# A hand-ordered prologue becomes one ordered by readiness, with its loads and eleven filler pieces regrouped

## The chip, the cores and the metric

The kernel runs on one core of one Trainium2 chip. The metric is the device time of one execution in microseconds (us); less is better. The core has a matrix engine (PE, whose weight loads are listed apart as PEld), a vector engine (DVE), an activation engine (ACT), a general engine (POOL) and a queue that issues most transfers (SP). Each engine works through its own instructions in the order fixed when the program is built, and waits where an operand is not there yet.

## The reference

x holds 32 sequences of 64 rows of 256; ctx_1024 holds 32 contexts of 1601 rows of 256. Six layers are added to x one after the other. Cut to what matters here:

```
x = x + L0_xattn(layernorm(x), ctx)   # x1 @ W1.T + (mean of ctx over its 1601 rows) @ W2.T + b
x = x + L0_attn(layernorm(x))         # attention of 64 by 64, 16 heads of 16, slopes * (j - i) added to the scores
x = x + L0_ffn(layernorm(x))          # shared gated network, and routed experts
x = x + L1_xattn(layernorm(x), ctx)   # 16 heads: softmax(q k^T / 4) v with k, v = Wk ctx + bk, Wv ctx + bv
x = x + L1_attn(layernorm(x))         # convolution, gated recurrence, gated network
x = x + L1_ffn(layernorm(x))          # ternary weights, 8-bit activations
```

Most of the work is in L1_xattn: each context row becomes a key and a value and is scored against 64 queries in 16 heads.

## The kernel before

**Tiles and pieces.** Two sequences make a tile of 128 rows, so there are 16 tiles (NT), taken in the order 1 to 15 and then 0. For L1_xattn each tile is split into 13 pieces (NU): per sequence (b) and per half of the channels (oc) three pieces of 512 context rows, and one piece with the 65 rows that are left of all four ("rest"). The main loop (L1463) runs over all 208 pieces g. One pass of it does, among others: `column_scores(g)` (L894, scores with context rows on partitions, exponential on ACT), `values(g + 3)` (L844), `row_scores(g + 5)` (L855, scores with queries on partitions, only to find the maxima, which DVE reduces, L871 and L874), `weighted(g)` (L924, the sum over values) and `keys(g + 6)` (L768, evicted by ACT with the bias added, L779 and L789). In the row-score order of a tile the rest piece comes first (number 0). `maxima` (L876) and `maxima_rows` (L887) turn the maxima of a half into a row of negative shifts that the column scores need. Between these, the layers of other tiles are run in small steps (generators that yield) from a plan with due times.

**Prologue.** Before the loop the first pieces must be there: keys 0 to 5, values 0 to 2, row scores 0 to 4, and for the row scores the query of the first tile, which needs the tile's whole first layer. `first()` (L1369) gives this chain in 27 steps: normalisation, the sums of two contexts (on ACT and DVE; L1377 to L1388), L0_xattn (xat, L359 to L365), L0_attn (transposed input tp_b, keys, queries and values, L375 to L403; scores, softmax, L408 to L433; weighted sum and wo, L446 to L479), L0_ffn (su, sv, lg, so, L486 to L505) and the query (tp_d, q, qbd, L746 to L764). Beside it stand the context sums of tiles 1 to 3 (`early_sums`, L1400: loads of 800 KB into two buffers "part", each summed by ACT), the second tile's first layer (`besides`, four effective steps), and the loads of the later weights (`late_weights`, L1247).

**What sets the order.** The prologue and the loop are inside `tc.manual_schedule` (L1430) for PE, DVE, ACT and POOL: there each engine's instructions stand in the order in which the program writes them. The prologue's order is a string of letters: a is one step of the chain, s of the sums, b of the second tile, k, v and r are keys, values and row scores of a piece, m and t the first maxima, w the late weights.

```
for what in """a a a a k1 a a k2 a a s s k3 k0 a a a a s s s s a k4 a v0 v1 a a a s s s s s s b a b a b a b a s w
               a s s a a a b a a s s s r b r b s s s r k5 b r m s s s r v2 t""".split():
    do[what]()
```

What is written outside that block (constants, masks, memsets, the first loads) and everything on SP is ordered on each engine by the compiler: among the instructions that its model takes to be ready, the one written first goes first.

**Buffers and queues.** PSUM has three single buffers for general results (mm_tile), two double ones for scores (sc_tile) and one for the weighted sums (o_tile). Key tiles have 7 buffers, contexts 2. The loads stand on SP's queue, in the text's order keys' weights, x, context 0, L0_xattn's weights, context 1 (two transfers), rest, eight weights; ACT's queue has the vectors chv, the rows (six bias rows and slopes, spread over 128 partitions) and the values' weights.

Of the kernel before, what the change touches and what calls it, by code (L numbers as in the profile page):

```python
# [15 lines left out]
P = 128  # L16
NB = 32
S = 64
# [26 lines left out]
def perceiver_kernel(ctx: ExitStack, tc: tile.TileContext, a: dict, out: bass.AP):  # L45
# [38 lines left out]
    def mm_tile(shape, name, dtype=F32):  # L84
        return home[0].mm.tile(shape, dtype, tag="mm", name=name)
# [38 lines left out]
    def load_rest(ti):  # L124

        t = big.tile([P, 2, 2, TAIL], F32, tag="rest", name=f"rest_{ti}", bufs=2)
        for b in range(2):
            nc.sync.dma_start(t[:, :, b, :], a["ctxT"][2 * ti + b].rearrange("(c p) l -> p c l", p=P)[:, :, NP * PIECE:])
        return t
# [2 lines left out]
    chv = const.tile([P, 2, len(CH)], F32, name="chv")  # L132
    nc.scalar.dma_start(chv, a["chv"])
    rows = const.tile([P, R_END], F32, name="rows")
    nc.scalar.dma_start(rows, a["rows"].partition_broadcast(P))

    ident = const.tile([P, P], F32, name="ident")
    make_identity(nc, ident)
# [26 lines left out]
    for hb in range(2):  # L165
        nc.gpsimd.iota(dist[hb * S:(hb + 1) * S, :], pattern=[[1, S]], base=0, channel_multiplier=-1,
                       allow_small_or_imprecise_dtypes=True)
    albi = const.tile([P, H, S], F32, name="albi")
    nc.vector.tensor_tensor(albi, rows[:, R_SL:R_SL + H].unsqueeze(2).to_broadcast([P, H, S]),
                            dist.unsqueeze(1).to_broadcast([P, H, S]), ALU.mult)  # L170


    gains = const.tile([P, 2, 3], F32, name="gains")
# [2 lines left out]
    def load_w(name, cols, chunks=2, eng=None):  # L176
        t = const.tile([P, chunks, cols], F32, name=f"w_{name}")
        (eng or nc.sync).dma_start(t, a[name].rearrange("(c p) o -> p c o", p=P))
        return t
# [588 lines left out]
    def keys(g):  # L768

        pos, h, k = scanned(g)  # L770
        if h is None:
            w = wholes[pos]
            w.kt = big.tile([P, 4, TAIL], F32, tag="ktr", name=f"ktr_{w.ti}", bufs=2)
            o = mm_tile([P, 2, 2 * TAIL], f"kps_{w.ti}")
            for oc in range(2):
                mmq2(o[:, oc, :], lambda c: w_k2[:, c, oc * P:(oc + 1) * P],
                     lambda c: w.rest[:, c].rearrange("p b l -> p (b l)"))
            for oc in range(2):
                nc.scalar.activation(w.kt.rearrange("p (b o) l -> p o b l", o=2)[:, oc],  # L779
                                     o[:, oc, :].rearrange("p (b l) -> p b l", b=2), AF.Identity,  # L780
                                     bias=chv[:, oc, BK2:BK2 + 1])
            return
        hf = halves[h]
        kt = big.tile([P, PIECE], F32, tag="kt", name=f"kt_{hf.name}_{k}", bufs=7)
        hf.kt.append(kt)
        o = mm_tile([P, PIECE], f"kps_{hf.name}_{k}")
        cT = ctxs[hf.batch]
        mmq2(o, lambda c: w_k2[:, c, hf.oc * P:(hf.oc + 1) * P], lambda c: cT[:, c, k * PIECE:(k + 1) * PIECE])
        nc.scalar.activation(kt, o, AF.Identity, bias=chv[:, hf.oc, BK2:BK2 + 1])  # L789
# [35 lines left out]

    def half_values(pos, h, k):
        v = value_tile([((pos, h, k), range(4))])
        o = mm_tile([P, 4, P], f"vps_{h}_{k}")
        cT = ctxs[h // 2]
        for j in range(4):  # L830
            k0 = k * PIECE + j * P
            mm2(o[:, j, :], lambda c: cT[:, c, k0:k0 + P], lambda c: w_v2[:, c, h % 2 * P:(h % 2 + 1) * P])
        values_out(v, o, P)
# [42 lines left out]
    def maxima(h):  # L876

        hf = halves[h]
        ng = small.tile([P, 4], F32, tag="ng", name=f"ng_{hf.name}")
        nc.vector.tensor_reduce(ng, wholes[hf.pos].mx[:, :, h % 4, :], AX.X, ALU.max, negate=True)  # L880
        m = mxp[h % 2]
        nc.vector.tensor_copy(m[:, :, 0], ng)
        nc.vector.tensor_tensor(ng, ng, m[:, :, 0], ALU.subtract)
        nc.vector.tensor_copy(m[:, :, 1], ng)
        nc.vector.tensor_tensor(m[:, :, 2], ng, m[:, :, 1], ALU.subtract)
# [327 lines left out]
    def load_batch(n):  # L1213
        hf = halves[2 * n]
        ctxs[n] = load_ctx(2 * hf.ti + hf.b, n == 1)


    w_k2 = load_w("L1_xattn_WkT", D)
    early_x[order[0]] = load_x(order[0])
    load_batch(0)  # L1220
    w_v2 = load_w("L1_xattn_WvT", D, eng=nc.scalar)
    w_xat = load_w("L0_xattn_WT", D, 4)
    load_batch(1)
    wholes[0].rest = load_rest(order[0])
    w_k = load_w("L0_attn_WkT", D)
    w_q = load_w("L0_attn_WqT", D)
    w_v = load_w("L0_attn_WvT", D)
# [129 lines left out]
    def first_layer(pos, k=0):  # L1357
        x3[pos] = yield from layer0(order[pos], csums.get(pos), k)
# [41 lines left out]
    def early_sums():  # L1400
        for pos in range(1, 4):
            yield from sums(pos, 2)
# [3 lines left out]
    def planned(gen, t0, t1, n, place):  # L1406
        plan.append(Steps(gen, t0 * NU / 16, t1 * NU / 16, n, place))
# [19 lines left out]
    planned(queried(NT - 1), 226, 231, 6, 2)  # L1427

    ET = mybir.EngineType
    with tc.manual_schedule(engines={ET.PE, ET.DVE, ET.Activation, ET.Pool}):  # L1430
        ahead, beside, summing = Steps(first()), Steps(first_layer(1, 1)), Steps(early_sums())

        def besides():
            if 1 in csums:
                beside.step()

        def scored():
            row_scores(scores.pop(0))

        scores = list(range(5))  # L1440
        do = {"a": ahead.step, "b": besides, "s": summing.step, "r": scored, "w": late_weights, "m": lambda: maxima(0),
              "t": lambda: maxima_rows(0)}
        do |= {f"k{g}": lambda g=g: keys(g) for g in range(6)} | {f"v{g}": lambda g=g: values(g) for g in range(3)}

        for what in """a a a a k1 a a k2 a a s s k3 k0 a a a a s s s s a k4 a v0 v1 a a a s s s s s s b a b a b a b a s w
                    a s s a a a b a a s s s r b r b s s s r k5 b r m s s s r v2 t""".split():
            do[what]()
        if beside.gen is not None:
            plan.insert(0, Steps(beside.gen, 0, 4, 28 - beside.done, 2))
        planned(biased(), 3, 5, 2, 1)  # L1450
        if summing.gen is not None:
            plan.insert(0, Steps(summing.gen, 0, 4.5, 37 - summing.done, 0))
        planned(all_ternary(), 5, 23, 24, 2)

        def run(t, place):
            for s in [s for s in plan if s.t0 <= t]:
                s.run(t, place)
                if t >= s.t1 and t < NU * NT - 1 and s.stop is None:
                    s.all()
                if s.gen is None:  # L1460
                    plan.remove(s)

        for g in range(NU * NT):  # L1463
            pos, p = divmod(g, NU)
            if pos + 1 < NT:
                if p == 0:
                    wholes[pos + 1].rest = load_rest(order[pos + 1])
                if p in (2, 9):
                    load_batch(2 * pos + 2 + p // 8)
            column_scores(g)  # L1470
            if g + 4 < NU * NT and scanned(g + 4)[2] == NP - 1:
                maxima_rows(scanned(g + 4)[1])
            if g == NU:
                more_values()
            if g + 3 < NU * NT:
                values(g + 3)
            if p == 1 and pos:
                normalise(pos - 1)
            if g == NU * NT - 2:
                normalise(pos, 3)  # L1480
            run(g, 0)
            if g + 5 < NU * NT:
                row_scores(g + 5)
                if scanned(g + 5)[2] == NP - 1:
                    maxima(scanned(g + 5)[1])
            run(g, 0.5)
            weighted(g)
            if p == NU - 1 and pos < NT - 1:
                gathered(pos)
            if p == 3 * NP and pos == NT - 1:  # L1490
                gathered(pos, 3)
            if g == NU * NT - 5:
                picked()
            in_columns[0] = True
            if g + 6 < NU * NT:
                keys(g + 6)
            if p == 1 and pos:
                x4[pos - 1] = projected(pos - 1)
            run(g, 1)
            in_columns[0] = False  # L1500
        normalise_last(NT - 1)
        x4[NT - 1] = projected(NT - 1)
        loop.close()
        late = []
        for k in range(2):
            late.append(Home(ctx.enter_context(tc.tile_pool(name=f"late{k}", bufs=2)),
                             ctx.enter_context(tc.tile_pool(name=f"late{k}s", bufs=3)),
                             ctx.enter_context(tc.tile_pool(name=f"late{k}m", bufs=3 - k, space=PSUM))))
        main = home[0]
        home[0] = late[0]  # L1510
        home[0].padded()
# [52 lines left out]
```

## Time and profile before

| | us |
|---|---|
| median of 3 runs | 2029.11 (2028.45 to 2029.33) |
| the profiled execution | 2027.19 |
| its span (first to last instruction) | 2025.5 |
| PE busy in the span | 1942.1 (96%) |
| DVE, ACT, POOL busy | 1295.2, 900.4, 326.4 |
| first column scores start | 77.4 |
| PE busy before that | 51.94 |

Times in the profile count from the span's start. The span is 1.7 us shorter than the execution's own time. A row of the timeline gives start, duration, engine, line, operation, what is written and from what, its shape and how many instructions were merged; in brackets stands how long the engine was idle before it and what ended the wait. PE's granted clock is given per stretch of time, 1.00 being full speed.

### The profile page before, as it was taken

How to read it: one execution, taken by the hardware profiler on the slowest of the kernel's cores; microseconds unless marked ns; L12 is line 12 of the kernel's file. 1: busy time of each engine (PE TensorE's matmuls, PEld its weight loads, DVE VectorE, ACT ScalarE, POOL GpSimd, SP SyncE). 2: the span in 40 equal slices, each digit the busy share in tenths (PEclk: the TensorE clock that was granted, in tenths of full speed). 3: DMA queues.
4: the chain of work that ended last, by engine and by line, in shares of the span. 5: the costliest groups of instructions: out<-in, count | busy, mean ns of one | idle time of the engine just before them, and what ended most of it. 6: DMA issues, size and time to landing. Idle time of an engine off the chain costs nothing. (4 is left out here: it accounts for less than half of the span.)

```text
span 2025.5 us, 76418 instructions
## 1 busy us (share of the span) xinstructions
PE 1942.1 (96%) x35143; PEld 1290.7 (64%) x35143; DVE 1295.2 (64%) x2618; ACT 900.4 (44%) x1400; POOL 326.4 (16%) x548
## 2 busy tenths in 40 slices
PE   6889999999999999999999999999999999999986
PEld 4556566667666666666666666666766666666664
DVE  4556766666656766666666766666666776656555
ACT  4345445454645444354544434444343433434342
POOL 2112111121111112111111111112111011100011
PEclk9899999999999999999999999999999999999998
DMA  9235323122232112121211111100111210111000
GB/s 310 78 117 168 122 86 112 48 79 84 89 99 87 56 48 73 66 78 64 72 48 54 43 50 40 50 28 25 35 51 45 81 45 2 48 47 38 13 10 8
DMA packets 54793, 136.68 MB, mean 67 GB/s; under 512 B 13318, under 2 KB 35016, under 8 KB 54472
## 3 DMA queue, kind: packets, MB, share of 16 engines
q1 hardware_dynamic: 53912, 130.99, 19.1%
q8 instruction: 275, 4.51, 0.9%
q10 hardware_dynamic: 560, 0.81, 0.2%
q14 instruction: 46, 0.38, 0.1%
HBM read 125.53 MB, written 6.25 MB: 65 GB/s over the span
## 5 line engine op out<-in xcount | busy, mean ns | idle before, releaser
L921 ACT ACTIVATE pt<-s 128x1024 f32<-128x1024 f32 (+1 forms) x416 | 403.1, 1020 | 266.6 <-PE s L915 266.4
L874 DVE TENSOR_REDUCE mx<-r 128x2 f32<-128x1024 f32 x384 | 451.8, 1219 | 97.1 <-PE r L867 96.8
L789 ACT ACTIVATE kt<-kps,chv 128x512 f32<-128x512 f32 x192 | 132.0, 687 | 581.9 <-PE kps L265 564.2
L253 PE MATMUL vps<-w_L_xattn_WvT,ctxT 128*128 128x256 f32 (+1 forms) x1632 | 380.4, 377 | 2.1 <-DVE y L1046 1.8
L265 PE MATMUL kps<-ctxT,w_L_xattn_WkT 128*32 128x512 f32 x2992 | 355.3, 592 | 0.0
L253 PEld LDWEIGHTS vps<-w_L_xattn_WvT,ctxT 128*128 128x128 f32 x1632 | 281.9, 190 | 48.3 <-issue 2.2
L867 PE MATMUL r<-kt,qbd 32*128 32x512 f32 x1536 | 231.5, 647 | 2.8 <-DVE mx L874 2.0
L814 DVE COPY vau<-vps 128x512 f32<-128x512 f32 x142 | 97.9, 690 | 203.5 <-PE vps L253 202.9
L940 PEld LDWEIGHTS o<-pt,vau 128*32 128x32 f32 (+1 forms) x9792 | 147.4, 110 | 97.4 <-issue 86.0
L915 PE MATMUL s<-qbd,kt 32*128 32x128 f32 x6144 | 208.1, 270 | 0.0
L915 PEld LDWEIGHTS s<-qbd,kt 32*128 32x128 f32 x6144 | 205.4, 186 | 3.0
L940 PE MATMUL o<-pt,vau 128*32 128x64 f32 (+1 forms) x9792 | 173.9, 221 | 3.8 <-ACT pt L921 3.5
L265 PEld LDWEIGHTS kps<-ctxT,w_L_xattn_WkT 128*32 128x32 f32 x2992 | 83.3, 110 | 112.0 <-issue 112.0
L867 PEld LDWEIGHTS r<-kt,qbd 32*128 32x128 f32 x1536 | 68.7, 184 | 46.4 <-issue 29.0
L909 PE MATMUL s<-neg,onesb 3*128 3x512 bf16 x768 | 82.4, 384 | 5.8 <-DVE mx L874 4.9
L909 PEld LDWEIGHTS <-onesb 3*128 3x128 bf16 x768 | 21.3, 91 | 104.0 <-issue 101.9
L814 DVE COPY part<-vps 128x512 f32<-128x512 f32 x50 | 34.5, 691 | 70.5 <-PE vps L253 70.3
L940 PEld LDWEIGHTS o<-pt,part 128*32 128x32 f32 (+1 forms) x3520 | 54.0, 110 | 34.9 <-issue 30.3
L311 ACT ACTIVATE part<-part 128x1601 f32<-128x1601 f32 x48 | 74.1, 1544 | 1.7 <-DMA part<-ctxT 1.7
L940 PE MATMUL o<-pt,part 128*32 128x64 f32 (+1 forms) x3520 | 65.4, 220 | 1.4 <-ACT nT L1054 0.7
L389 POOL TENSOR_TENSOR kbd<-kT,mask 128x512 f32<-128x512 f32 x32 | 32.6, 1040 | 114.0 <-ACT kT L382 114.0
L253 PE MATMUL ff<-nT,w_fg 128*128 128x128 f32 x384 | 48.7, 276 | 2.3 <-DVE fm L274 1.6
(391 smaller groups left out, 2517.5 us busy)
## 6 DMA issues: line engine op xcount, KB each, us to landing
ctxT<-ctxT SPq DMA_DIRECT2D x31, 1601.0 KB
part<-ctxT SPq DMA_DIRECT2D x60, 800.5 KB
od<-osb SPq DMA_DIRECT2D x15, 256.0 KB
rest<-ctxT SPq DMA_DIRECT2D x32, 65.0 KB
x<-x SPq DMA_DIRECT2D x16, 128.0 KB
out<-x SPq DMA_DIRECT2D x16, 128.0 KB
w<-w SPq DMA_DIRECT2D x16, 128.0 KB
rs<-od SPq DMA_DIRECT2D x30, 64.0 KB
```

Of the source, the lines that this page charges most:

```text
L253: nc.tensor.matmul(o, lhsT=lhsT(c), rhs=rhs(c), start=(c == 0), stop=(c == 1))
L265: nc.tensor.matmul(o[r], lhsT=lhsT[:, r], rhs=rhs, start=start, stop=stop)
L311: nc.scalar.activation(parts[j], parts[j], AF.Copy, accum_out=csum[:, c, 2 * i + b:2 * i + b + 1])
L389: nc.gpsimd.tensor_tensor(kbd[oc], kT[:, oc, :].rearrange("p (b k) -> p b k", b=2).unsqueeze(2).to_broadcast([P, 2, 4, S]), mask4.unsqueez ...
L789: nc.scalar.activation(kt, o, AF.Identity, bias=chv[:, hf.oc, BK2:BK2 + 1])
L814: nc.vector.tensor_copy(v[:kr, :, 0:VW - 16].rearrange("p k (h d) -> p k h d", d=17)[:, :, :, 0:16], o[:kr].rearrange("p k (h d) -> p k h ...
L867: nc.tensor.matmul(o, lhsT=qbd[r, q % 2, q // 2].rearrange("p h q -> p (h q)"), rhs=w.kt[r, q, :] if h is None else halves[h].kt[k][r, :], ...
L874: nc.vector.tensor_reduce(w.mx[:, 2 * m:2 * m + 2, h % 4, k], ps[m], AX.X, ALU.max)
L909: nc.tensor.matmul(o, lhsT=onesb[r, :], rhs=halves[h].neg[r, :].unsqueeze(1).to_broadcast([3, 4, P]), start=True, stop=False)
L915: nc.tensor.matmul(ps[i // 2][:kr, i % 2, j * P:(j + 1) * P], lhsT=w.kt[r, j, :] if h is None else halves[h].kt[k][r, j * P:(j + 1) * P], ...
L921: nc.scalar.activation(pt[:kr].rearrange("p i k c -> p i (k c)"), ps[m][:kr], AF.Exp)
L940: nc.tensor.matmul(w.o[32 * c:32 * c + 32, q, m, :], lhsT=v[:kr, i, 17 * hd:17 * hd + 32], rhs=pts[m][:kr, c // 2, j, c % 2 * S:c % 2 * S ...
```

## The change

The prologue's steps are written ahead of `tc.manual_schedule`, so that they are ordered by readiness, and the loop alone stays in the hand-ordered block. In the text the whole chain (27 steps) stands first, then keys 1, 2, 3, 0, 4, 5, values 0 to 2, row scores 0 and 1, keys 6, row scores 2, keys 7, row scores 3, the first maxima; then 13 steps of the sums, 4 of the second tile, the late weights and 9 more steps of the sums. Keys 6 and 7 are new in the prologue and left out of the first two passes of the loop. Row scores 4 move into the first pass, ahead of `weighted(0)`, which now stands ahead of row scores 5. Keys before piece 6 use the score buffers instead of the general ones, and values 0 to 2 the buffer of the weighted sums. The first loads are x, context 0, L0_xattn's weights, context 1, then the keys' weights, the rows but for their first 256 columns (which stay on ACT's queue), the values' weights (moved from ACT's queue to SP's) and the rest; albi, the table of slopes times distances, is computed after these in the text.

```
-    nc.scalar.dma_start(rows, a["rows"].partition_broadcast(P))
+    nc.scalar.dma_start(rows[:, 0:R_BO], a["rows"][0:R_BO].partition_broadcast(P))
...
-            o = mm_tile([P, 2, 2 * TAIL], f"kps_{w.ti}")
+            o = sc_tile(f"kps_{w.ti}")[:, :, :2 * TAIL] if g < 6 else mm_tile([P, 2, 2 * TAIL], f"kps_{w.ti}")
...
-        o = mm_tile([P, PIECE], f"kps_{hf.name}_{k}")
+        o = sc_tile(f"kps_{hf.name}_{k}")[:, 0] if g < 6 else mm_tile([P, PIECE], f"kps_{hf.name}_{k}")
...
-        o = mm_tile([P, 4, P], f"vps_{h}_{k}")
+        o = o_tile([P, 4, P], f"vps_{h}_{k}") if 3 * h + k < 3 else mm_tile([P, 4, P], f"vps_{h}_{k}")
...
-    w_k2 = load_w("L1_xattn_WkT", D)
     early_x[order[0]] = load_x(order[0])
     load_batch(0)
-    w_v2 = load_w("L1_xattn_WvT", D, eng=nc.scalar)
     w_xat = load_w("L0_xattn_WT", D, 4)
     load_batch(1)
+    w_k2 = load_w("L1_xattn_WkT", D)
+    nc.sync.dma_start(rows[:, R_BO:], a["rows"][R_BO:].partition_broadcast(P))
+    w_v2 = load_w("L1_xattn_WvT", D)
     wholes[0].rest = load_rest(order[0])
+    albi = const.tile([P, H, S], F32, name="albi")
...
+    for what in """a a a a a a a a a a a a a a a a a a a a a a a a a a a k1 k2 k3 k0 k4 k5 v0 v1 v2 r r k6 r k7 r m t
+                s s s s s s s s s s s s s b b b b w s s s s s s s s s""".split():
+        do[what]()
...
     with tc.manual_schedule(engines={ET.PE, ET.DVE, ET.Activation, ET.Pool}):
...
             run(g, 0)
+            if g == 0:
+                scored()
+                weighted(g)
             if g + 5 < NU * NT:
                 row_scores(g + 5)
...
-            weighted(g)
+            if g:
+                weighted(g)
...
-            if g + 6 < NU * NT:
+            if 7 < g + 6 < NU * NT:
                 keys(g + 6)
```

More of the change, by code (lines that the diff above doesn't have):

```diff
@@ L167, in perceiver_kernel @@
                        allow_small_or_imprecise_dtypes=True)
-    albi = const.tile([P, H, S], F32, name="albi")
-    nc.vector.tensor_tensor(albi, rows[:, R_SL:R_SL + H].unsqueeze(2).to_broadcast([P, H, S]),
-                            dist.unsqueeze(1).to_broadcast([P, H, S]), ALU.mult)
     gains = const.tile([P, 2, 3], F32, name="gains")
@@ L1215, in load_batch @@
         ctxs[n] = load_ctx(2 * hf.ti + hf.b, n == 1)
-    w_k2 = load_w("L1_xattn_WkT", D)
     early_x[order[0]] = load_x(order[0])
     load_batch(0)
-    w_v2 = load_w("L1_xattn_WvT", D, eng=nc.scalar)
     w_xat = load_w("L0_xattn_WT", D, 4)
     load_batch(1)
+    w_k2 = load_w("L1_xattn_WkT", D)
+    nc.sync.dma_start(rows[:, R_BO:], a["rows"][R_BO:].partition_broadcast(P))
+    w_v2 = load_w("L1_xattn_WvT", D)
     wholes[0].rest = load_rest(order[0])
+    albi = const.tile([P, H, S], F32, name="albi")
+    nc.vector.tensor_tensor(albi, rows[:, R_SL:R_SL + H].unsqueeze(2).to_broadcast([P, H, S]),
+                            dist.unsqueeze(1).to_broadcast([P, H, S]), ALU.mult)
     w_k = load_w("L0_attn_WkT", D)
@@ L1429, in perceiver_kernel, with besides, scored @@
     ET = mybir.EngineType
-    with tc.manual_schedule(engines={ET.PE, ET.DVE, ET.Activation, ET.Pool}):
[L1431 to L1453, printed above, removed]
+    ahead, beside, summing = Steps(first()), Steps(first_layer(1, 1)), Steps(early_sums())
+    def besides():
+        if 1 in csums:
+            beside.step()
+    def scored():
+        row_scores(scores.pop(0))
+    scores = list(range(5))
+    do = {"a": ahead.step, "b": besides, "s": summing.step, "r": scored, "w": late_weights, "m": lambda: maxima(0),
+          "t": lambda: maxima_rows(0)}
+    do |= {f"k{g}": lambda g=g: keys(g) for g in range(8)} | {f"v{g}": lambda g=g: values(g) for g in range(3)}
+    for what in """a a a a a a a a a a a a a a a a a a a a a a a a a a a k1 k2 k3 k0 k4 k5 v0 v1 v2 r r k6 r k7 r m t
+                s s s s s s s s s s s s s b b b b w s s s s s s s s s""".split():
+        do[what]()
+    if beside.gen is not None:
+        plan.insert(0, Steps(beside.gen, 0, 4, 28 - beside.done, 2))
+    planned(biased(), 3, 5, 2, 1)
+    if summing.gen is not None:
+        plan.insert(0, Steps(summing.gen, 0, 4.5, 37 - summing.done, 0))
+    planned(all_ternary(), 5, 23, 24, 2)
+    with tc.manual_schedule(engines={ET.PE, ET.DVE, ET.Activation, ET.Pool}):
         def run(t, place):
```

## The prediction

> **What bounds the kernel now.** I read the page first (engine shares, then the 40 slices), then a table of busy time by stage, then the first 130 us in order of time, then the waits. The slices (about 50.6 us each) show PE at 6 and 8 tenths in the first two and 9 until the last two: the kernel is bound by PE except in a prologue and a tail. The diff touches only the prologue and the first two pieces of the loop. The table by stage (PE, PEld, DVE, ACT, POOL busy, then the granted clock, DMA share and GB/s) is cut at the loop's first column scores (77.4) and the next three:
>
> ```profile
> 0.00:77.40 77.40, 51.94 (x299) 31.95 (x300) 39.30 (x76) 28.05 (x46) 15.03 (x42) 0.82 0.72 243
> 77.40:89.30 11.90, 11.22 (x169) 8.02 (x169) 4.30 (x7) 3.51 (x6) 1.84 (x4) 1.00 0.01 3
> 89.30:98.40 9.10, 9.10 (x191) 5.94 (x191) 5.04 (x8) 4.07 (x6) 2.83 (x3) 1.00 0.28 92
> 111.00:1950.00 1839.00, 1808.55 (x33736) 1199.06 (x33736) 1195.06 (x2393) 834.30 (x1282) 287.65 (x468) 1.00 0.19 62
> ```
>
> The loop is 98% PE (1808.55 of 1839) and stays as it is. So the change is worth (1) how much earlier the first column scores start and (2) what the first two pieces gain or lose. What ends last before 77.4 is one chain: contexts loaded and summed, tile 0's first layer, its query, row scores, maxima, first column scores. Its PE steps (start, duration), with idle time ahead in brackets:
>
> ```profile
> 11.91 3.75 PE L261 MATMUL kps<-ctxT,w_L_xattn_WkT 128*128 128x512 f32 x4 [11.91 <-DMA ctxT<-ctxT]
> 19.74 1.13 PE L261 MATMUL xat<-w_L_xattn_WT,mT 128*128 128x256 f32 x4
> 43.52 2.08 PE L253 MATMUL su<-xT_c,w_L_ffn_sw1T 128*128 128x128 f32 x8 [0.46 <-ACT xT_c L243]
> 48.32 2.05 PE L261 MATMUL so<-w_L_ffn_sw2T,m 128*128 128x256 f32 x4 [0.37 <-PE lg L261]
> 56.71 2.08 PE L867 MATMUL r<-ktr,qbd 32*128 32x65 f32 x32 [0.45 <-DVE qbd L761]
> 59.58 2.68 PE L867 MATMUL r<-kt,qbd 32*128 32x512 f32 x8 [0.79 <-DVE mx L871]
> 62.98 3.20 PE L867 MATMUL r<-kt,qbd 32*128 32x512 f32 x8 [0.72 <-DVE mx L874]
> 66.11 3.55 PE L261 MATMUL kps<-ctxT,w_L_xattn_WkT 128*128 128x512 f32 x4
> 72.27 2.26 PE L867 MATMUL r<-kt,qbd 32*128 32x512 f32 x8 [1.32 <-DVE mx L874]
> 74.45 2.05 PE L253 MATMUL vps<-w_L_xattn_WvT,ctxT 128*128 128x128 f32 x16
> ```
>
> Two things are to be seen. Durations double where PE was idle before: a key piece is 3.75 at 11.9 and 3.55 at 66, but 1.88 at 20.7; the granted clock reads 0.50 from 42 to 69. And behind the query (56.7) the hand order still puts a key piece (66.11) and a value piece (74.45) into the chain.
>
> **A. Start of the chain.** It is gated by the second context's sums:
>
> ```profile
> 17.30 0.99 DVE L1387 TENSOR_REDUCE csum<-ctxT 128x1 f32<-128x801 f32 x1 [3.69 <-DMA ctxT<-ctxT]
> ```
>
> Ahead of and with that load the kernel requests 4892 KB (14 + 524 rows + 256 keys' + 256 values' weights + 128 x + 1601 + 512 + 1601). After the change 3984 KB: 908 KB fewer (396 of the rows, 256, 256). At the 374 GB/s of 10 to 20 us that is 2.5 us. ACT's last part sum began 0.91 us after the landing, because an eviction and a copy stood before it; with the keys gone from there, that goes too. So xat could start at 19.74 - 3.4 = 16.3. But no keys have warmed PE: four matmuls of that shape take 2.05 cold (so) against 1.13, +0.9. **A = -2.5.** Ends: -3.4, if PE is warm; +0.4, if the first key piece (its weights land 0.7 us later, at 15.5) is queued whole ahead of xat (15.5 + 3.75 = 19.25, plus 0.9). I lean to the early end: xat needs 1.5 us after the landing. The rows' remainder, the values' weights and albi (1.22 us of DVE, at 7.9 now) move to a time when DVE waits for loads; both DMAs stand ahead of the layer weights on SP's queue, 652 KB or 1.8 us, and those are first read 5 us after xat: nothing.
>
> **B. xat to query (20.98 to 56.71).** *Gain:* all keys and three values are now fillers behind the chain, ordered by readiness: 7 x 1.88 + 1.06 + 3 x 2.05 = 20.4 us of PE work. Chain work on PE from xat to tp_c is 9.2 us, cold start 3: together 16.3 + 32.6 = 49, so PE can stay busy and warm until so. Warm prices are the second tile's: su to lg takes 1.89 there (116.12 to 118.01) against 3.57, so 1.03 (xat's row) against 2.05, transpose and query 1.6 against 2.74. Gain 1.7 + 1.0 + half of 1.15 = 3.3. *Loss:* the hand order let the chain wait for almost no filler; an order by readiness starts a filler just before the chain's next step is ready. PE: 12 entries, half meet a 0.47 us matmul, half of it left: 1.4. ACT: 8 evictions of 0.69 and about 3 sums of 1.73 are 10.7 us in 36, 30%; 8 entries x 0.3 x 0.45 = 1.1. **B = -3.3 + 2.5 = -0.8**; ends -3.8 (all warm, no delay) and +5.5 (each of the eight evictions ahead of a step). Key pieces now evict from the score buffers and values from the output buffer, idle until the loop: nothing, and if one is late it is a filler that is late.
>
> **C. Query to first column scores (56.71 to 77.42, 20.7 us).** Gone from here: the key piece, the fifth row scores, the value piece. I replay the rest with the cold rows: row scores start 56.71, 59.58, 62.98; the next needs the first maximum of the third (ends 66.3) instead of following the key piece at 69.8. Their second maxima end 4.5 us after the start, as in the 62.98 row (67.46): 70.8. Five small maxima 1.0, transpose 0.2 plus copy and gaps 0.5: column scores at 72.5. **C = -4.9.** If PE were warm, four row scores at the 2.46 spacing of 69.81 to 72.27 would give -9.4; if both key pieces stay between row scores, as the text has them, 0.
>
> **D. First pieces.** Two key pieces leave (1.90 each) and one row scores comes in (1.14). That looks like -2.7, but the rows of the first piece say otherwise:
>
> ```profile
> 83.55 2.34 DVE L874 TENSOR_REDUCE mx<-r 128x2 f32<-128x1024 f32 x2
> 84.34 1.90 PE L265 MATMUL kps<-ctxT,w_L_xattn_WkT 128*32 128x512 f32 x16
> 85.80 0.41 DVE L219 TENSOR_SCALAR xn_b<-x,mv_b,rstd_b 128x256 f32<-128x256 f32 x1
> 86.35 0.41 PE L237 MATMUL tp_b<-ident,xn_b 128*128 128x128 f32 x2
> ```
>
> The keys end when xn_b does; xn_b waits for the maxima on DVE. Taking the keys out only bares this wait, and the added row scores put another 2.36 us of maxima ahead of xn_b on DVE's queue, behind which the second tile's transpose, keys and queries stand: +2.4. In the second piece the next column scores wait 0.74 for a maximum even with the keys there: their removal gives 0. Last, PE enters the loop cold; now it was warm from 69.2 (62.98 to 69.2 dense at half clock: at most 3.1 us lost). I take a third, +1.0, since the maxima cover part. **D = +3.4**; ends 0 and +5.5.
>
> **Sum:** -2.5 - 0.8 - 4.9 + 3.4 = -4.8. Against the profiled execution (2027.19, span 2025.5): 2022.4. The median of the runs shown is 1.9 above that execution: **2024.3**.
>
> *A rule weighed.* Rows: su, sv and lg are dense from 43.52 to 47.95 and stay at 0.50; PE warms only at 69.2, after 6.2 dense us. The Trainium skill ("TensorE: Matmul & The Clock Gate", Part 1) says that the clock comes up after about 3.4 us of sustained work. By it the row scores would run warm from the second on, C would be near its -9.4 and the time near 2020; the rows contradict it here, so I don't use it.
>
> **Rivals.** *1. Waits for loads inside the chain (slower).* Outside the hand-ordered block the order is fixed when the program is built, from assumed times; an engine then waits in that order. It is already seen to be wrong:
>
> ```profile
> 7.23 0.43 DVE L209 BATCH_NORM_STATS2 st_a<-x 128x6 f32<-128x256 f32 x1 [1.69 <-DMA x<-x]
> 7.79 0.19 DVE L140 CAST identb<-ident 128x128 bf16<-128x128 f32 x1
> ```
>
> and, from the waits of SP's queue between 18 and 60 us (total, times, longest):
>
> ```profile
> SPq L112 <- ACT part L281: 27.0, 6, 8.0
> ```
>
> identb, ready since 1.5, stands behind a wait for x; SP's queue stood up to 8.0 us for a sum that was assumed done. If one sum stands on ACT ahead of a chain step while its load is queued behind the late weights (2846 KB, 8.3 us at 350 GB/s) and one part (2.3 us), the chain loses 10.6: 2034.9. From 4.8 us lost the kernel is slower than before. Against it: the 8.0 us show compute assumed too early against SP's queue, which would put sums late on ACT, not early. *2. PE stays warm through the row scores:* C = -9.4 and no cold entry (-1.0): 2018.8. For it: 20.4 us of fillers. Against: little is left after 49. *3. Wash:* B at +4: 2029, if fillers delay every step. *4. Not what it says:* order as written, keys and values (16.5 us) after the query: about +13, 2042. Against: identb shows that instructions do move.
>
> **Chances.** Forecast (2021 to 2027) 0.42, warm 0.24, waits 0.22, wash 0.08, as written 0.04. Faster by over 0.2% (4.06 us, about what a measurement of this kernel can tell from no change) takes 0.28 of the forecast and the warm case: 0.52. Within: 0.14 and 0.06 of the wash: 0.20. Slower: 0.28. Range 2015 to 2036: from the warm case with B at its good end (2018.8 - 3.0 = 2015.8) to the waits case and a little over it.
>
> **What would show it.** A: xat on the sums at 16 to 17.5. B: su at 2.1 or 1.16, ACT and PE rows just ahead of each chain step. C: four row scores, no keys between, column scores near 70. D: xn_b of the second tile 2.4 later after the column scores than now (8.4). Wrong, if an ACT, DVE or PE row in 15 to 60 waits for part, or if the loop after the fourth piece takes another time.

## The result, and the profile after

The changed kernel takes **2033.34 us** (median of 22 runs, 2026.79 to 2039.93) beside 2029.38 us of the kernel before (22 runs, 2024.69 to 2034.05). The ratio is 1.0018, 95% interval 1.0011 to 1.0026: some 3.7 us slower. The forecast was 2024.3, 4.8 us faster. The direction is wrong; the time lies inside the range (2015 to 2036).

The profiled execution of the changed kernel took 2038.79 us (span 2037.1). That is 5.4 above its median, as single executions of both kernels scatter by 5 to 7 us to either side; so I compare stages, not ends. First the table by stage (PE, PEld, DVE, ACT, POOL busy, granted clock, DMA share, GB/s), cut at the first two column scores, then the stretch that turned out to matter, and the long rest of the loop:

```profile
0.00:72.59 72.59, 47.47 (x300) 28.88 (x301) 33.72 (x74) 27.29 (x45) 14.09 (x42) 0.92 0.72 248
72.59:90.30 17.71, 15.26 (x159) 11.42 (x159) 6.72 (x9) 3.31 (x6) 2.64 (x5) 0.79 0.01 2
119.50:129.00 9.50, 9.45 (x102) 7.02 (x106) 3.91 (x7) 0.76 (x2) 0.00 (x0) 0.51 0.74 277
119.00:1958.00 1839.00, 1811.65 (x33645) 1200.19 (x33647) 1191.96 (x2385) 829.98 (x1277) 286.05 (x463) 0.99 0.19 62
```

The first column scores come 4.8 us earlier (72.59 against 77.42). But the first piece takes 17.71 us instead of 11.90, at a clock of 0.79 instead of 1.00, and further on PE runs 9.5 us almost without a gap at half speed. The chain's PE steps in order of time (start, duration), with two rows of DVE and ACT that bear on them, idle time ahead in brackets:

```profile
16.13 0.29 DVE L352 TENSOR_SCALAR mT<-csum 128x256 f32<-128x256 f32 x1
16.69 1.91 PE L258 MATMUL kps<-ctxT,w_L_xattn_WkT 128*128 128x512 f32 x2
18.39 1.66 PE L258 MATMUL xat<-w_L_xattn_WT,mT 128*128 128x256 f32 x4
...
42.96 1.54 ACT L278 ACTIVATE part<-part 128x1601 f32<-128x1601 f32 x1 [1.50 <-DMA part<-ctxT]
44.90 1.16 PE L250 MATMUL su<-xT_c,w_L_ffn_sw1T 128*128 128x128 f32 x8 [0.67 <-ACT xT_c L240]
...
55.01 1.91 PE L258 MATMUL kps<-ctxT,w_L_xattn_WkT 128*128 128x512 f32 x2
56.85 1.27 PE L864 MATMUL r<-ktr,qbd 32*128 32x65 f32 x32
...
63.75 3.54 PE L258 MATMUL kps<-ctxT,w_L_xattn_WkT 128*128 128x512 f32 x4
67.22 1.23 PE L864 MATMUL r<-kt,qbd 32*128 32x512 f32 x8
71.94 0.29 PE L887 MATMUL tpm<-identb,mxp 128*128 128x128 bf16 x1 [3.49 <-DVE mxp L882]
```

Key pieces stand in the chain in two places: half of one ahead of xat, though xat's operand mT was ready at 16.4, and the added pieces 6 (in two halves, the first ahead of all row scores) and 7 between the row scores. Then PE waits 3.5 us for the last maxima, and the column scores start cold.

The first piece, as it looks on DVE and PE from 78 on:

```profile
78.07 1.03 PE L258 MATMUL xat<-w_L_xattn_WT,xT_a 128*128 128x256 f32 x4
...
81.07 4.81 DVE L871 TENSOR_REDUCE mx<-r 128x2 f32<-128x1024 f32 x4
85.80 0.40 DVE L216 TENSOR_SCALAR xn_b<-x,mv_b,rstd_b 128x256 f32<-128x256 f32 x1
86.26 0.44 PE L234 MATMUL tp_b<-ident,xn_b 128*128 128x128 f32 x2 [1.65 <-DVE xn_b L216]
...
88.45 1.91 PE L250 MATMUL q<-xT_b,w_L_attn_WqT 128*128 128x128 f32 x8
```

Two row scores' maxima (four, 4.81 us) stand ahead of the second tile's xn_b where one's (2.34) stood, PE waits, and q behind it is cold again (1.91; warm it takes 1.06). The fourth piece, first as it was before the change and then after it:

```profile
114.17 1.54 ACT L281 ACTIVATE part<-part 128x1601 f32<-128x1601 f32 x1
...
116.12 1.16 PE L253 MATMUL su<-xT_c,w_L_ffn_sw1T 128*128 128x128 f32 x8 [1.67 <-ACT xT_c L243]
```

```profile
116.09 1.54 ACT L278 ACTIVATE part<-part 128x1601 f32<-128x1601 f32 x1
...
117.61 1.54 ACT L278 ACTIVATE part<-part 128x1601 f32<-128x1601 f32 x1
...
119.13 0.37 ACT L240 COPY xT_c<-tp_c 128x256 f32<-128x256 f32 x1
119.55 2.08 PE L250 MATMUL su<-xT_c,w_L_ffn_sw1T 128*128 128x128 f32 x8 [3.06 <-ACT xT_c L240]
```

Two context sums stand on ACT ahead of xT_c where before there was one, so PE waits 3.06 us (before 1.67), and comes back at half clock for 9.5 us.

### The profile page after: what moved, and what is told of

It is laid out like the page before. It is cut to its first block, busy times and chain, and to the rows that moved or that the text cites. A ratio compares the mean times of both kernels' runs of the same rounds, so it can differ in the third digit from the quotient of the medians.

```text
span 2037.1 us, 76361 instructions
## 1 busy us (share of the span) xinstructions
PE 1952.3 (96%) x35119; PEld 1300.1 (64%) x35119; DVE 1292.5 (63%) x2618; ACT 901.0 (44%) x1400; POOL 326.2 (16%) x548
```

## The experiments

**Theory 1, the first pieces.** The prologue gains what its rows show (some 4 to 5 us) and the first four pieces give it back: the first through the cold clock and the maxima ahead of xn_b, the fourth because the new string has 22 sum steps and not 24. Three steps make one sum: 8 stand ahead of the loop in the profile of before and 7 in that of after, so one more is left to the plan for the first pieces. **Theory 2, the loop.** The whole loop became slower, since keys and values come from other buffers and run at another distance. **Theory 3, readiness.** The compiler's order itself costs, whatever the text.

To measure stages I use the start of the first exponential of each of the loop's first pieces; a piece lasts from one to the next. In the profile of before the first stands at 78.7, and the pieces take 11.9, 10.1, 11.6, 16.8, then 10.3, 9.1, 9.0, 7.6. From the fifth piece to the 21st every profile below has before's steps to 0.1 us, so "shift" is the distance to before's profile there. Later, single pieces differ by up to 2.4 us in every profile, some up and some down: after's distance falls from 7.8 to 4.2 (88th piece) and ends at 9.7. The fall is common to the eight profiles with keys 6 and 7 ahead of the loop, whose 22nd, 61st and 87th pieces are together 3.4 us shorter than before's; no run shows why. So a shift measures the first pieces and not the whole time. Against theory 2 speaks e1, whose loop is after's: it is 1.5 us behind before at the fifth exponential and 1.5 at the last.

| kernel | first exp. | 1st piece | 4th piece | shift | median (runs) | ratio to before, 95% |
|---|---|---|---|---|---|---|
| after | 75.0 | 17.5 | 22.7 | +7.8 | 2033.34 (22) | 1.0018 [1.0011, 1.0026] |
| e1_sums | 74.5 | 17.1 | 16.8 | +1.5 | 2029.80 (11) | 0.9996 [0.9985, 1.0008] |
| e2_warm | 72.8 | 16.0 | 19.9 | +2.7 | 2033.68 (12) | 1.0009 [1.0000, 1.0018] |
| e3_r4 | 78.5 | 15.3 | 22.8 | +9.6 | 2034.91 (10) | 1.0018 [1.0008, 1.0027] |
| e4_k67 | 74.8 | 15.0 | 19.8 | +2.2 | 2033.59 (11) | 1.0009 [0.9997, 1.0020] |
| e5_best | 73.2 | 12.6 | 16.8 | -2.9 | 2024.11 (11) | 0.9974 [0.9962, 0.9986] |
| e12_again | 73.4 | 12.6 | 16.8 | -2.6 | 2022.20 (6) | 0.9959 [0.9945, 0.9972] |
| e6_text | 104.0 | 17.5 | 22.8 | +37.2 | 2067.91 (1) | |
| e7_ready | 81.1 | 11.9 | 16.8 | +2.4 | 2034.99 (10) | 1.0024 [1.0013, 1.0035] |
| e8_sums_k67 | 74.7 | 15.0 | 16.8 | -0.9 | 2029.40 (10) | 0.9991 [0.9980, 1.0002] |
| e9_loads | 76.7 | 17.5 | 16.8 | +4.2 | 2034.49 (10) | 1.0025 [1.0012, 1.0037] |
| e10_xn | 73.6 | 13.5 | 16.8 | -2.8 | 2026.59 (12) | 0.9983 [0.9972, 0.9994] |
| e11_xn_k67 | 73.9 | 16.4 | 16.8 | -0.4 | 2029.72 (12) | 0.9995 [0.9985, 1.0005] |

The median of before beside these runs lies between 2029.25 and 2031.52, so kernels are compared by their ratios. e6 is a single execution.

**e1_sums: the two missing sum steps, and with them the eighth sum, put back.**

```
-                s s s s s s s s s s s s s b b b b w s s s s s s s s s""".split():
+                s s s s s s s s s s s s s b b b b w s s s s s s s s s s s""".split():
```

> The changed kernel with two more steps of the context sums in the prologue (24 as before the change, not 22); nothing else. Theory 1 (first pieces): the changed kernel starts its first column scores 4.8 us earlier, loses 5.8 us in the first piece and 5.9 us in the fourth, where two sums of 1.73 us stand on ACT ahead of the second tile's xT_c copy and PE then runs at 0.5 from 119.5 to 129. With one sum there as before, su starts about 1.7 us earlier, the clock stays up, and the time falls by 4 to 6 us against the changed kernel, to about 2028. Theory 2 (the loop): the loop as a whole is slower after the change (PE busy 1952.3 against 1942.1), the fourth piece is chance: no fall, ratio to before stays near 1.0018.

The fourth piece is back at 16.8, with one sum ahead of xT_c and su warm:

```profile
115.63 1.54 ACT L278 ACTIVATE part<-part 128x1601 f32<-128x1601 f32 x1
...
117.57 1.16 PE L250 MATMUL su<-xT_c,w_L_ffn_sw1T 128*128 128x128 f32 x8 [1.54 <-ACT xT_c L240]
```

The ratio falls from 1.0018 to 0.9996. Two letters in a string are some 4.5 us, by the two intervals give or take 3: as much as the whole loss against before. The same edit on e4 (it gives e8, below) is worth 3.7 by the ratios. The first piece stays at 17.1, as it should.

**e2_warm: PE kept at work while DVE finds the last maxima.** Four matmuls of 128x512 whose result is read by nothing stand between the last row scores and m.

```
+    def dummies():
+        o = mm_tile([P, PIECE], "dummy")
+        kt7 = halves[scanned(7)[1]].kt[scanned(7)[2]]
+        for i in range(4):
+            nc.tensor.matmul(o, lhsT=kt7[:, 0:P], rhs=ctxs[0][:, 0, 0:PIECE], start=True, stop=True)
+    do["d"] = dummies
-    ... r r k6 r k7 r m t
+    ... r r k6 r k7 r d m t
```

> The changed kernel with four extra matmuls of 128x512 whose result nothing reads (lhsT the key tile of piece 7, so they can't run before 68 us), placed on PE between the fourth row scores and the first maxima's transpose, where PE now waits 3.5 us. Theory 1: PE enters the loop at full clock; of the first piece's +5.8 the cold part, 2.3 (scores, values) and 1.1 (keys and queries) us, goes, less 0.3 for the matmuls: about -3 us against the changed kernel, and the first piece lasts 14.4 instead of 17.7 us. Theory 2: the first piece gets shorter too, but the time stays: ratio to before near 1.0018. Were the extra matmuls themselves late, +1 us.

The column scores run warm, and the second piece starts 3.8 us earlier against before than in the changed kernel (-2.0 instead of +1.8). From the column scores (71.46) to xn_b (82.30) it takes 10.84 us: 13.21 in after, 8.38 before, so what is left over before is the added maxima, 2.5, and the 2.4 gone were the clock. But the first piece takes 16.0, not 14.4, since behind the wait for xn_b PE is cold once more (k 2.08). The fourth piece shows that its size hangs on the clock: the same two sums ahead of xT_c and the same wait of 3.06, but 19.9 instead of 22.7, since the clock is back at 1.00 by 122.

**e3_r4: the fifth row scores back into the prologue.**

```
-    ... r r k6 r k7 r m t
+    ... r r k6 r k7 r m t r
...
             if g == 0:
-                scored()
                 weighted(g)
```

> The changed kernel with the fifth row scores back in the prologue, after the first maxima (r at the end of r r k6 r k7 r m t r), and out of the first piece. Theory 1: the second tile's xn_b then waits for one row scores' maxima instead of two: 2.4 us less in the first piece; the first column scores wait for the score buffers, 1 to 2.4 us later; and PE enters the loop a little warmer. Net -2 to 0 us against the changed kernel. If the first piece's loss is not DVE's maxima but only the clock, xn_b stays 13 us behind the first column scores.

The first piece gains 2.2 us, as expected, but the first exponential comes 3.6 us later, more than expected: the compiler puts the row scores (71.74) ahead of the maximum's transpose (74.91), and their maxima on DVE among the five small steps to it. By the shift the move into the loop was worth 1.8 us, by the ratios nothing (1.0018 both); what it lacked was a place behind xn_b on DVE (see e10).

**e4_k67: keys 6 and 7 back in the loop.**

```
-    ... r r k6 r k7 r m t
+    ... r r r r m t
...
-            if 7 < g + 6 < NU * NT:
+            if g + 6 < NU * NT:
```

> The changed kernel with the keys of pieces 6 and 7 left in the first two passes of the loop, as before the change, and out of the prologue. Theory 1: keys 6 and 7 cost the prologue about 1.1 us before the first row scores and up to 3.5 us before the fourth (63.75 to 67.3, cold), and save the first two pieces nothing, since these wait for DVE: first column scores 2 to 3 us earlier, net -3 to -1 us. If the keys taken out do shorten the first pieces by 1.9 us each, net 0 to +2 us.

Here I missed. Without the key pieces the row scores follow each other, but at half clock, and the column scores come at 72.4 as with them. First one of the row scores, then the stretch's sums:

```profile
62.79 3.21 PE L864 MATMUL r<-kt,qbd 32*128 32x512 f32 x8 [0.72 <-DVE mx L871]
```

```profile
56.50:72.00 15.50, 11.40 (x58) 5.13 (x59) 9.99 (x16) 0.00 (x0) 0.00 (x0) 0.50 0.19 61
```

The two key pieces in the chain thus pay for themselves there: what they take, the warm clock gives back to the row scores. In the loop, key piece 6 fills the wait for xn_b, k and q run warm (1.16 and 1.06), and the first piece is 2.5 shorter; 0.9 of that came earlier, as the clock was back sooner at the values (2.47 against 3.40). **e8_sums_k67**, e1 and e4 together, adds up:

> The changed kernel with 24 steps of the sums and with keys 6 and 7 left in the loop (two of the earlier edits together). Theory 1: the pieces' steps add up: first piece 15.0 as with keys 6 and 7 in the loop alone, fourth piece 16.8: pieces after the fourth start 0.9 us before those of the kernel before, ratio 0.9990 to 1.0000. If the fourth piece's loss hangs on something else than the two sums, it stays at 19.8.

**e10_xn: xn_b ahead of the second row scores.** e1, and the second tile's next step written right behind the first weighted sum, so that on DVE only one row scores' maxima stand ahead of it.

```
             if g == 0:
                 scored()
                 weighted(g)
+                second.step()
```

> The changed kernel with 24 steps of the sums and xn_b of the second tile ahead of the fifth piece's row scores, without the extra matmuls; to be read between the run with the sums alone (first piece 17.1) and the one with all three edits (12.6). If DVE's second maxima cost the 2.4 us that the prediction gave them, the first piece lasts 14 to 15 us, the pieces after the fourth start about 1 us before those of the kernel before, ratio 0.9985 to 0.9997; the rest of the difference to 12.6 is the clock's. If the clock is all, the first piece stays at 17.

```profile
79.40 2.36 DVE L871 TENSOR_REDUCE mx<-r 128x2 f32<-128x1024 f32 x2
...
81.67 0.40 DVE L216 TENSOR_SCALAR xn_b<-x,mv_b,rstd_b 128x256 f32<-128x256 f32 x1
81.99 2.35 DVE L871 TENSOR_REDUCE mx<-r 128x2 f32<-128x1024 f32 x2
82.87 0.44 PE L234 MATMUL tp_b<-ident,xn_b 128*128 128x128 f32 x2
```

First piece 13.5 instead of 17.1, and faster than before (0.9983). The maxima cost 2.4; the other 1.2 is the clock, which the shorter wait no longer loses (k and q in 1.16 and 1.06, in e1 1.60 and 1.91).

**e5_best and e12_again: e10 and the spare matmuls.**

> The changed kernel with three edits at once: two more steps of the sums in the prologue, the four extra matmuls (their result is not read), and in the first piece one step of the second tile (xn_b) ahead of the fifth piece's row scores, so that xn_b waits for one row scores' maxima on DVE instead of two. Theory 1 (first pieces): first column scores 6 us before those of the kernel before (as with the extra matmuls alone), first piece 13 to 14 us instead of 16.0, fourth piece 16.8: the pieces after the fourth start 3 to 5 us earlier than before the change, and the time is 3 to 5 us below it, ratio 0.9975 to 0.9985. Theory 2 (the loop is slower as a whole): ratio at 0.9995 or more whatever the pieces show.

> The kernel with 24 sum steps, four spare matmuls ahead of the maximum's transposes (their result is read by nothing) and the early scaling, a second time beside the others on one chip: theory of the first pieces expects 0.996 to 0.9985 again, and that it lies within 0.1% of the one with the keys in the loop; were the first time an accident of the executions' scatter, it would lie within 0.1% of the kernel before.

```profile
67.94 3.70 PE L1449 MATMUL dummy<-ctxT,kt 128*128 128x512 f32 x8
```

In e12 the spare matmuls end as the maxima do, the maximum's transpose follows at 71.49 without a wait, and the column scores are warm (1.07 against 1.92). First piece 12.6; 0.9974 and 0.9959. This is the fastest version by its medians, 5 to 8 us below before: the changed prologue keeps a gain once the first and the fourth piece are mended. How much of it the spare matmuls bring is not shown. The 0.9 us by which the first piece is shorter than e10's goes again in the third (12.6 and 12.8 against 11.4), the shifts are the same (-2.9 and -2.6 against -2.8), and the intervals of e5 and e10 overlap. e12 also missed in one thing: it lies 0.4% below e11, the kernel with the keys in the loop, and not within 0.1% of it.

**e11_xn_k67: e10 with keys 6 and 7 in the loop.**

> The changed kernel with 24 sum steps in its string, the second tile's scaling (xn_b) issued right behind the first column scores' weighting, and keys 6 and 7 left in the loop's passes. Theory of the first pieces: the two gains lie on the same path, VectorE's queue behind the first column scores, so they add only in part: first column scores' exponential at 74 to 75, first piece 11.5 to 13.5 us (13.5 with the early scaling alone, 15.0 with the keys alone), fourth piece 16.8, ratio 0.997 to 0.999. Theory that the whole loop is slower: 1.000 to 1.003.

A miss: 16.4 and 0.9995. The clock stays at half from 56.5 to 77, so that xn_b comes 1.2 us later behind the column scores than in e10, and with xn_b early the key piece no longer fills a wait but makes one:

```profile
82.69 0.41 DVE L216 TENSOR_SCALAR xn_b<-x,mv_b,rstd_b 128x256 f32<-128x256 f32 x1
83.89 1.92 PE L262 MATMUL kps<-ctxT,w_L_xattn_WkT 128*32 128x512 f32 x16
85.74 0.44 PE L234 MATMUL tp_b<-ident,xn_b 128*128 128x128 f32 x2
```

So in the first piece the moves depend on each other: with xn_b late the keys belong in the loop (15.0 against 17.1), with xn_b early ahead of it (13.5 against 16.4).

**e9_loads: e1 with the loads in the old order.** The three lines of w_k2, w_v2 and rows stand as before.

> The changed kernel with 24 steps of the sums and with the first loads as before the change (keys' weights first, the rows whole and the values' weights on ACT's queue); to be read against the run with the sums alone (first column scores' exponential at 74.5, ratio 0.9996). If the loads in the chain's order are worth what the prediction gave them, the second context lands at 17 instead of 14.8 and xat on the sums starts about 2 us later; keys then warm PE early, which gives back up to 1 us: first column scores 1 to 2.5 us later, ratio 1.000 to 1.001. If the order of the loads is hidden (keys between x's and the sums' part of xat take what it gives), no difference within 0.5 us.

The loads' order is worth 2.2 us at the first exponential (76.7 against 74.5): the second context's DVE sum starts at 16.95 and not at 14.75. The ratio, 1.0025, lies above the range that I expected; by the shift the order is worth 2.7 us, by the ratios 5.9.

**e6_text and e7_ready: text and readiness apart.** e6 puts the changed prologue back inside `tc.manual_schedule`; e7 takes before's prologue out of it and changes nothing else.

> The changed kernel with its prologue back inside the hand-ordered block, so that its steps run in the order of the text: chain first, keys and values only after the query. This is the prediction's rival 4. Theory 1: the query is reached a few us earlier (no filler ahead of a chain step: about 2.5 us of filler waits gone, but PE cold, 3 to 4 us more on su, so, q), then about 16.5 us of keys and values stand before the row scores: first column scores at 85 to 90, time about +10 to +15 us. If readiness gave nothing, first column scores stay near 73.

> The kernel before with one thing changed: its prologue, letters and loads as they are, stands ahead of the hand-ordered block, so that it is ordered by readiness. It still has 24 steps of the sums, five row scores in the prologue and keys 6 and 7 in the loop. Theory 1: first column scores between 73 and 77, first piece 12 to 15, fourth piece 16.8; the pieces after the fourth start 3 us earlier to 1 us later than before: ratio 0.9985 to 1.0005. If ordering by readiness is itself what costs (fillers ahead of the chain), first column scores after 78 and ratio above 1.001.

As written, the new text is 29 us worse than when ordered by readiness (first exponential 104.0 against 75.0). Behind the query five whole key pieces, the rest's keys and three value pieces stand ahead of any row scores (74.99, in after 56.85); the first three of them:

```profile
56.35 6.77 PE L258 MATMUL kps<-ctxT,w_L_xattn_WkT 128*128 128x512 f32 x12
```

The column scores then start at 91.7, somewhat later than I expected (85 to 90), and what I had not counted comes behind them: all seven sums stand on ACT between the last keys (83.57) and the first exponential, some 10 of the 29 us.

And before's text is 2.4 us worse by readiness than by hand, 4.9 by the ratio, where I had expected a gain or little change. Theory 3 holds for the old text and fails for the new one. The loads are not what makes the difference: the new text with the old loads (e9) has its first exponential at 76.7, the old text at 81.1. Whether it is the chain's place at the head of the text or the other buffers was not isolated.

## Why the prediction was wrong

| step | predicted | measured | up to |
|---|---|---|---|
| A | -2.5 | -0.9 | x (20.98 to 20.09) |
| B | -0.8 | +1.0 | first row scores (56.71 to 56.85) |
| C | -4.9 | -5.0 | first column scores (77.42 to 72.59) |
| D | +3.4 | +5.8 | second column scores (89.29 to 90.30) |
| second and third piece | 0 | +0.9 | fourth exponential (112.4 to 114.3) |
| fourth piece | no term | +5.9 | fifth exponential (129.1 to 137.0) |

**Two steps failed most.** *The cold entry in D ("I take a third, +1.0").* From the column scores to xn_b the wait grew by 4.8 (8.38 to 13.21): 2.5 for the added maxima, as forecast, and 2.4 for PE, whose column scores and values are cold (xat starts 5.5 behind the column scores, before 3.1). From xn_b to the second column scores another 1.0 went, since PE cools down in the wait ahead of k and q. So 3.4 and not 1.0; e2 confirms the split. The 0.9 of the next row is the same cold clock: 0.8 of it lies between the second column scores and their exponential. *That the loop "stays as it is".* I counted the string's keys, values and row scores and passed over its s: 24 before, 22 after. The sum not finished ahead of the loop stands on ACT in the plan, and it landed ahead of xT_c: 1.5 us of wait, and some 4.4 for the clock that it lost (9.5 us at 0.51). By e1 this step alone turns no change into slower.

**A** lost 1.6 to half a key piece ahead of xat, between the two ends that I gave (warm, or a whole piece); the landing came 2.5 earlier, as counted. **B**: su to lg ran warm as forecast (su 1.16), but the chain waited more. Half of key piece 6 held the row scores back by 1.2 us: qbd starts 1.0 earlier than before (55.25), the row scores 0.1 later. And xT_c stood behind a sum that itself waited 1.50 for its load (42.96), so that PE waited 0.67 for it ahead of su: the prediction's sign of rival 1, a row that waits for part, but at 0.7 us where I had priced 10.6. **C** has the right number by luck. My replay has cold row scores and no keys between them; in the run both added key pieces stand between, for which I had put C at 0, and the row scores are warm. The replay itself was sound: e4, without these keys, has its column scores at 72.4 where it gave 72.5. And that the loop gains nothing by the keys' leaving was too kind: e4's first piece is 2.5 shorter with key piece 6 in it.

**Rivals.** Slower came out, by a mechanism that no rival names. Rival 2 came half true: three of the four row scores at 1.23 to 1.55, bought with the key pieces, and a cold entry all the same. Rival 3 asked for B at +4; it was +1.0. Rival 4 is out by e6.

*The rule weighed.* The Trainium skill ("TensorE: Matmul & The Clock Gate", Part 1) has PE come up after some 3.4 us of sustained work. I set it aside by before's rows. In after, q and half a key piece (53.14 to 56.85, 3.7 us) are cold and the row scores behind them warm, which agrees with the rule; from 119.5 to 129 PE was busy 9.45 of 9.50 us and stayed at 0.51, which does not.

**What stays open.** The trace has +7.8 at the fifth piece, the ratio says +3.7. The 3.4 us that the loop takes back by the 88th piece would go far to close this, but the trace loses more again behind it. The profiled execution is the second slowest of its 22, and the fourth piece took 22.7 or 22.8 in three of five profiles with 22 sum steps and 19.8 or 19.9 in two, by how soon the clock came back; how often each happens in the other executions is not known. In the loop, too, single pieces lose up to 1.7 us where the clock drops (0.58 from 1852 to 1856 in after), which blurs every comparison of ends. Nor is it isolated which matmuls keep the clock up.

## What to carry to other kernels

When a prologue is rewritten, count every kind of step ahead of the loop against the old one: what is missing comes back as queued work in the loop, at a place that nobody chose. Price a wait on the matrix engine with the clock that it loses: 1.4 us more of waiting cost 5.9 in the changed kernel, and 3.0 to 6.0 in the other profiles with that wait. And a filler in the chain is judged by what stands behind it: taking the same two key pieces out of the loop cost 2.1 us of the first piece where the vector engine's queue ended the wait (e8 to e1), and saved 2.9 where the matrix engine did (e11 to e10).

## What the runs showed of the hardware

Work that is nearly dense does not always bring the clock up: 3.7 us of 128x128 matmuls did (53.14 to 56.85 in after), 4.4 us of su, sv and lg did not (43.52 to 47.95 in before, 0.50), nor did 9.5 us of mixed forms (0.51 in after, PE busy 9.45). With gaps, 15.5 us of mostly 32-row row scores did not either (0.50 in e4, PE busy 11.40). A wait of 1.54 us for xT_c left the clock up in e1 (su 1.16), one of 3.06 did not (2.08). And the scatter of single executions goes with the mean granted clock: of e5's eleven the fastest has 0.993 (2020.60) and the slowest 0.987 (2028.55).
